# Column sums of the feed-forward and gate weights: other tiles than the ring of convolution accumulators

## The chip, the cores and the metric

The kernel runs on one core of a Trainium2 chip. The metric is the device time of one execution in microseconds (us). A core has five engines with their own instruction streams: TensorE (PE, matrix products; the loading of its weights is shown apart as PEld), VectorE (DVE), ScalarE (ACT), GpSimd (POOL) and SyncE (SP, which issues the transfers here). They wait for each other through semaphores. Tiles live in SBUF, results of PE in PSUM.

## The reference

A decoder layer on `x` of 16 sequences, 256 tokens, 512 features, all float32, in three blocks, each followed by a layer norm over the features:

1. A state-space block: RMS norm, one input projection to `z` (1024), `xi` (1024), `dt` (16), `B` and `C` (256 each); a causal depthwise convolution of four taps on `xi` and SiLU; the mean of `xi` in each of 16 heads; a linear recurrence over tokens with 16 states per head; a projection of its 16 outputs to 1024, gated by `silu(z)`; an output projection to 512 and the residual.
2. A long convolution: for each of 32 groups of 8 positions, products of `x` with a context are convolved with a kernel of 512 lags (in the reference by FFT), weighted with the context again and summed.
3. A feed-forward block: `base = x @ W.T + b`, plus a low-rank update of the two best of 8 experts, weighted by a softmax of gate logits `x @ gate_w.T + gate_b`.

What the change touches prepares block 3:

```python
base = x_flat @ W.T + b
logits = x_flat @ gate_w.T + gate_b
...
xA = jnp.einsum('nd,erd->ner', x_flat, lora_A)
...
out = base + SCALING * lora_update
```

The input of block 3 is a layer norm. The kernel multiplies weights whose column means have been subtracted with the input that is not yet normalised, so that the mean of the input drops out; the residual is in the weights too, as an added identity.

## The kernel before

The kernel has two parts. The first (blocks 1 and its norm) goes through 8 groups of 512 tokens, `g` from 0 to 7. The second (blocks 2 and 3) goes through 32 heads of positions. Instructions run on every engine in the order in which the program gives them; [...]the framework only adds the waits. A tile with a tag takes a slot in the ring of that tag; if all slots of the ring are held, the first writer of the new tile waits until the last reader of the slot's old tile is done.

In a group, ten pairs of output chunks of the input projections are computed one after another (`order`: `x`, `z`, `x`, `x`, `z`, `x`, `b`, `c`, `z`, `z`), each in seven half-size products (L328). Step `i` of the loop begins the products of pair `i` and ends those of pair `i-1`. After a pair of `xi` chunks is complete, `mixed` (L578 to L582) convolves its two chunks: the first tap of an even chunk on DVE (L580), of an odd chunk on ACT (L578), the three further taps on DVE (L582). The result is a tile with the tag `acc`, a ring of six slots of 128 x 512 float32; SiLU is applied in place later (L637). At `i == 6`, `head_means` (L593) multiplies the first four of these tiles into a PSUM tile `xm`.

PSUM tiles for various purposes share the tag `tr` with two banks: `xm`, the row `mw` of column means below, the outputs `yps` of the recurrence and others.

In group 1, between these steps, the weights of block 3, loaded at the end of group 0, are prepared: at `i == 2` DVE adds the identity to `w_f` (L518, L520); at `i == 3` POOL sums the four row blocks of `w_f` (512 columns), at `i == 4` those of `w_gl` (136 columns), both in `chunk_sum` (L525, L527); at `i == 5` and `i == 6`, `centred` multiplies a sum with a constant matrix on PE, which gives the column means in all partitions (L533), and DVE subtracts them from the four row blocks (L535):

```python
if g == 1 and i in (3, 4):
    w, cols = ((w_f, D), (w_gl, NE + ER))[i - 3]
    total = chunk_sum(w, cols)
if g == 1 and i in (5, 6):
    centred(*sums.pop(0))
```

In the kernel before, the two sums are tiles of the ring `acc`, beside the convolution's tiles.

Another ring is named here by the change: the tag `vn` of the pool `q3`, a single slot of 128 x 512 float32. In the first part it holds `yT`, the outputs of the recurrence, written by ACT near the end of each group (L700) and read by PE as weights (L735); in the second part it holds the loaded `vn` (L137 on). The pool `p1` has one slot for each of its tiles.

## Time and profile before

| | |
|---|---|
| median of 3 runs | 1436.82 us (1436.52 to 1436.96) |
| the profiled execution | 1436.9 us |
| its span, first to last instruction | 1435.1 us |
| mean granted clock of PE | 0.996 |
| PE busy | 1415.7 us (99% of the span) |
| DVE busy | 1209.7 us (84%) |
| ACT busy | 438.1 us (31%) |
| POOL busy | 470.6 us (33%) |
| chain that ended last | PE 96%, DVE 2%, issue 1%, POOL 1% |

Busy time is the sum over an engine's instructions; registers, branches and semaphores are not in it. The chain that ended last is followed back from the last instruction: at each step to what released it, or to the instruction before it on its engine. The granted clock is the share of PE's full rate that was let through. A time in a view is counted from the first instruction of the span; a line such as L535 is a line of the kernel before, and in the changed kernel lines from 525 on stand three lines further down.

### The profile page before, as it was taken

Reading aid. Unit: us, or ns where it says so; the run is one execution under the profiler, and the core shown is the slowest. Engines: PE = TensorE matmul, PEld = TensorE weight load, DVE = VectorE, ACT = ScalarE, POOL = GpSimd, SP = SyncE. Lnnn points to the kernel's source line nnn. Section 1 sums busy time; section 2 is a strip of 40 time slices with the busy share of each in tenths; the row PEclk is TensorE's granted clock in tenths of the full one; section 3 lists DMA queues with packets and bytes.
Section 4 is the critical chain, followed back from the end, with each engine's and each line's share of the span. In section 5 each row is a group of like instructions: output and inputs, shape, how many; then the busy total and the mean of one; then the engine's idle time right before and its main releaser. Section 6 shows DMA issues by size and latency. Waiting matters only on the chain.

```text
span 1435.1 us, 19011 instructions
## 1 busy us (share of the span) xinstructions
PE 1415.7 (99%) x6944; PEld 914.7 (64%) x6944; DVE 1209.7 (84%) x2102; ACT 438.1 (31%) x962; POOL 470.6 (33%) x661
## 2 busy tenths in 40 slices
PE   9999999999999999999999999999999999999997
PEld 7887788888888888888884444444444444444443
DVE  6988788878788787877847999999999999999996
ACT  2423223233232232332311333233323333333331
POOL 5452010010100201001003564556455545554552
PEclk9999999999999999999999999999999999999999
DMA  8114021120121111212003112221221122112200
GB/s 299 33 39 130 8 63 65 37 83 8 39 81 45 54 36 38 83 34 94 16 16 107 63 47 74 67 64 55 70 71 61 58 66 74 54 65 66 74 27 23
DMA packets 49166, 89.18 MB, mean 62 GB/s; under 512 B 8880, under 2 KB 13360, under 8 KB 49072
## 3 DMA queue, kind: packets, MB, share of 16 engines
q1 hardware_dynamic: 49072, 87.96, 19.2%
q8 instruction: 55, 0.90, 0.3%
q14 instruction: 39, 0.32, 0.1%
HBM read 70.62 MB, written 17.32 MB: 61 GB/s over the span
## 4 chain that ended last, share of the span: by engine, by line
PE 96%; DVE 2%; issue 1%; POOL 1%; DMA 0%; ACT 0%; POOLq 0%; SPq 0%; DVEq 0%
PE mm L328 20%; PE y L1021 15%; PE s L328 14%; PE y L1036 12%; PE base L1196 7%; PE s L778 6%; PE mm L778 6%; PE y L1006 4%; PE gl L1272 2%; PE base L1192 2%; PE tr L1108 1%; PE tr L145 1%; PE xm L593 1%; PE mm L735 1%; PE mm L869 1%; PE s L869 1%
## 5 line engine op out<-in xcount | busy, mean ns | idle before, releaser
L1071 DVE TENSOR_TENSOR pr<-y,cT 128x1024 f32<-128x1024 f32 x126 | 148.2, 1217 | 47.1 <-PE y L1036 47.1
L1036 PE MATMUL y<-kv 64*64 64x512 f32 x1536 | 179.6, 598 | 0.0
L582 DVE SCALAR_TENSOR_TENSOR acc<-xi,wc,acc 128x512 f32<-128x512 f32 x192 | 142.0, 753 | 9.8 <-ACT acc L578 4.1
L1081 DVE TENSOR_REDUCE red<-pr 128x128 f32<-128x1024 f32 x126 | 147.1, 1208 | 0.0
L155 DVE TENSOR_TENSOR kv<-tr,cT 128x1024 f32<-128x1024 f32 x124 | 145.4, 1213 | 0.0
L1021 PE MATMUL y<-kv 128*128 128x512 f32 x272 | 128.2, 594 | 0.6 <-ACT y L1010 0.4
L1036 PEld LDWEIGHTS y<-kv 64*64 64x64 f32 x1536 | 52.2, 132 | 119.0 <-issue 96.9
L1196 PE MATMUL base<-w_f,ol 128*128 128x512 f32 x248 | 121.4, 593 | 0.0
L1021 PE MATMUL y<-kv,Td 128*128 128x512 f32 x248 | 116.5, 592 | 0.0
L66 POOL TENSOR_TENSOR rs_a<-ve_a,nhalf 128x1 f32<-128x1 f32 x32 | 19.0, 594 | 243.0 <-DVE ve_a L64 243.0
L389 POOL TENSOR_TENSOR rstd<-ms,nhalf 128x4 f32<-128x4 f32 (+1 forms) x9 | 8.5, 948 | 258.9 <-DVE ms L387 258.9
L1021 PEld LDWEIGHTS y<-kv 128*128 128x128 f32 x272 | 51.1, 190 | 66.4 <-issue 48.9
L1229 POOL TENSOR_TENSOR ol<-o,red 128x512 f32<-128x512 f32 x31 | 39.4, 1272 | 161.7 <-DVE red L1081 161.7
L328 PE MATMUL mm<-XT,w_z 128*128 128x256 f32 x384 | 90.7, 379 | 0.0
L1021 PEld LDWEIGHTS y<-kv,Td 128*128 128x128 f32 x248 | 47.1, 190 | 59.3 <-issue 59.3
L991 POOL TENSOR_TENSOR xs<-kv 128x512 f32<-128x512 f32 x63 | 80.2, 1274 | 2.4
L1010 ACT COPY y<-y 64x512 f32<-64x512 f32 x124 | 69.2, 558 | 34.7 <-PE y L1006 28.9
L328 PEld LDWEIGHTS mm<-XT,w_z 128*128 128x128 f32 x384 | 73.0, 190 | 9.9
L328 PE MATMUL mm<-xnT,w_z 128*128 128x256 f32 x288 | 71.0, 382 | 0.0
L1006 PE MATMUL y<-xs,kv 128*128 128x512 f32 x124 | 64.8, 604 | 2.6 <-DVE pr L1071 1.6
L1196 PEld LDWEIGHTS base<-w_f,ol 128*128 128x128 f32 x248 | 42.5, 190 | 30.9 <-issue 30.9
L328 PE MATMUL s<-XT,w_xi 128*128 128x256 f32 x256 | 61.0, 380 | 0.6 <-DVE XT L224 0.5
(278 smaller groups left out, 2827.3 us busy)
## 6 DMA issues: line engine op xcount, KB each, us to landing
cT<-in_ctxT SPq DMA_DIRECT2D x32, 384.0 KB
kv<-in_toep SPq DMA_DIRECT2D x32, 384.0 KB
xt<-in_x SPq DMA_DIRECT2D x32, 256.0 KB
spread<-both SPq DMA_DIRECT2D x32, 256.0 KB
first<-xt SPq DMA_DIRECT2D x32, 256.0 KB
vn<-first SPq DMA_DIRECT2D x32, 256.0 KB
out<-res SPq DMA_DIRECT2D x31, 256.0 KB
xnT<-in_xT SPq DMA_DIRECT2D x7, 1024.0 KB
```

Source lines behind the costliest of these rows:

```text
L155: last = nc.vector.tensor_tensor(kv[:, q, k * BQ : (k + NL // 2) * BQ], vT[:, q, blks].rearrange("p k (b i) -> p (k b) i", i=NH).unsqueeze ...
L328: nc.tensor.matmul(ps, w[:, p, a, kc, :], Xs[b][:, kc, :], start=start and kc == 0, stop=stop and kc == 1, skip_group_check=upon,)
L582: ins = nc.vector.scalar_tensor_tensor(acc, xi[:, :, k : k + S], wc[:, c, k : k + 1], acc, ALU.mult, ALU.add)
L778: nc.tensor.matmul(ps, own[a][c][:, n * P : (n + 1) * P], w_o[b][c], start=start and c == 0, stop=stop and c == HC - 1, skip_group_check=upon,
L991: return nc.gpsimd.tensor_tensor(xs[:, q], moving(kv, q, 0), moving(kv, q, 1), ALU.add)
L1006: nc.tensor.matmul(bank_of(y, 3), T[:, SHARED_AT, :], xs[:, q], start=True, stop=True)
L1010: nc.scalar.copy(bank_of(y, 2)[b : b + HP], bank_of(y, 3)[a : a + HP])
L1021: nc.tensor.matmul(bank_of(y, lb), w, moving(kv, q, mb), start=not late and lb not in begun, stop=False, skip_group_check=True,)
L1036: return nc.tensor.matmul(bank_of(y, lb)[cols], T[rows, DIAGONAL_AT, (b - a) * HP : (b - a + 1) * HP], moving(kv, q, lb)[rows], start=star ...
L1071: nc.vector.tensor_tensor(pr.rearrange("p (k b j) i -> p k b j i", k=2, j=NH), y[i].rearrange("p k (b j i) -> p k b j i", j=NH, i=NH), cT[ ...
L1081: nc.vector.tensor_reduce(red[:, q, 2 * i : 2 * i + 2, :].rearrange("p k t -> p (k t)"), pr, AX.X, ALU.add)
L1196: nc.tensor.matmul(base, o_l[:, kc, :], w_f[:, kc, :], start=(first and kc == kcs[0]), stop=False)
```

## The change

`chunk_sum` no longer takes its tile from the ring `acc` of the pool `p2`. The sum of `w_f` (512 columns) becomes a tile of the one-slot ring `vn` in the pool `q3`, the sum of `w_gl` (136 columns) a tile of its own, `g_sum`, in the pool `p1`. Nothing else is edited.

```diff
         def chunk_sum(w, cols):
 
-            total = p2.tile([P, D], F32, tag="acc", name="w_sum", bufs=6)[:, 0:cols]
+            if cols == D:
+                total = q3.tile([P, D], F32, tag="vn", name="w_sum", bufs=1)
+            else:
+                total = p1.tile([P, cols], F32, name="g_sum")
             nc.gpsimd.tensor_tensor(total, w[:, 0, :], w[:, 1, :], ALU.add)
             for kc in range(2, KD):
                 nc.gpsimd.tensor_tensor(total, total, w[:, kc, :], ALU.add)
```

## The prediction

> **What bounds the kernel now.** I read the page's busy shares first: TensorE (PE) is busy 99% of the 1435.1 us span and the granted clock averages 0.996. A change that moves no matmul can therefore only win PE idle time or PE time at a lowered clock. The table of waits says where PE idle time is large enough to matter. In it, "A <- B: total, times, longest" means that A waited for B (first line from the whole span, the others from 100 to 175 us):

> ```profile
> PE xm L593 <- DVE w_f L535: 5.6, 1, 5.6
> ACT acc L578 <- PE mw L533: 5.7, 1, 5.7
> DVE acc L582 <- ACT acc L578: 2.3, 1, 2.3
> ```

> One single PE wait of 5.6 us, in token group 1. The chain that ended last, in order of time (start, us, what), shows how it arises:

> ```profile
> 140.80 0.25 PE mw L533 x2
> 141.05 0.02 issue
> 141.07 0.73 ACT acc L578
> 141.80 0.02 issue
> 141.82 0.77 DVE acc L582
> ...
> 144.15 2.40 DVE w_f L535 x4
> 146.55 0.04 issue
> 146.59 1.93 PE xm L593 x8
> 148.53 4.94 PE s L328 x16
> 153.47 6.04 PE mm L328 x28
> ...
> 240.78 1.00 PE xm L593 x8
> 241.78 3.65 PE s L328 x16
> 245.43 6.04 PE mm L328 x28
> ```

> Read upwards: the head means `xm` need a bank of the two-deep ring `tr`, which is held by the column mean of `w_f` until VectorE (DVE) has subtracted it (L535). L535 stands on DVE behind the convolution of chunk 5 (L582), whose first tap ScalarE (ACT) computes (L578). And that tap waited until the matmul on the sum of `w_gl` had read the ring slot the tap writes into. The DVE timeline (start, us, line, idle before it) prices the detour:

> ```profile
> 136.64 0.48 DVE L580 TENSOR_SCALAR acc<-xi,wc 128x512 f32<-128x512 f32 x1
> 137.15 2.33 DVE L582 SCALAR_TENSOR_TENSOR acc<-xi,wc,acc 128x512 f32<-128x512 f32 x3
> 141.82 2.33 DVE L582 SCALAR_TENSOR_TENSOR acc<-xi,wc,acc 128x512 f32<-128x512 f32 x3 [2.34 <-ACT acc L578]
> 144.07 2.47 DVE L535 TENSOR_TENSOR w_f<-w_f,mw 128x512 f32<-128x512 f32 x4
> ```

> The last view is busy time by stretch (PE first, PEclk in the third column from the right):

> ```profile
> 144.00:144.25 0.25, 0.00 (x0) 0.00 (x0) 0.25 (x2) 0.07 (x1) 0.00 (x0) 1.00 0.00 0
> 144.31:144.50 0.19, 0.00 (x0) 0.00 (x0) 0.19 (x1) 0.19 (x1) 0.00 (x0) 0.50 0.00 0
> 150.90:151.05 0.15, 0.15 (x2) 0.15 (x1) 0.00 (x0) 0.00 (x0) 0.00 (x0) 0.50 0.00 0
> 151.15:151.30 0.15, 0.15 (x2) 0.15 (x1) 0.00 (x0) 0.00 (x0) 0.00 (x0) 1.00 0.00 0
> ```

> So the stall has a second price: the clock is half from 144.28 to 151.11 us. In group 2 the matmuls from `xm` to the 28 `mm` take 245.43 - 240.78 = 4.65 us, in group 1 153.47 - 146.59 = 6.88. The halved clock costs 2.23 us after the stall's 5.6.

> **The change, part by part.** Times are of the profiled execution (1436.9 us, span 1435.1; the runs' median is 1436.82, 0.1 less). Instruction streams of both kernels are the same in number, kind and order on every engine and in the DMA queue; only waits differ.

> 1. *Work.* Three POOL additions for `w_f`, three for `w_gl`, two column-mean matmuls and eight subtractions stay as they are: 0.
> 2. *Taken away: the wait of chunk 5's tap.* Its input, `xi`, is ready at 136.31 + 0.41 = 136.72. The tap takes 0.72, so it is done at about 137.5. DVE gets to it after the three L582 of chunk 4. Six L582 in a row take 4.48 us where nothing stops them (130.19 to 134.67, the next start), so L535 starts at 137.15 + 4.48 = 141.63 instead of 144.07: 2.44 earlier. `xm` follows at 144.15 instead of 146.59. PE's stall falls from 5.56 (its timeline) to 3.12 us. It does not vanish: DVE itself, which has not been idle since 127.42 apart from this wait, is now what is late.
> 3. *Clock.* The window 140.87 to 144.28 still holds only 0.16 us of PE work before the stall and 0.13 after it, 8%, well below the 33% that lowered the clock elsewhere. I take it that the clock still falls at 144.28. But the window 144.28 to 147.69 is now full[...], so half clock lasts 3.41 us, not 6.83. The loss is 3.41 / 2 = 1.71 instead of 2.23: 0.52 more. The two unknowns, whether a window at 8% counts as idle and whether the next restores, bound this part between 0 and 3.41 us of loss, that is from +2.23 to -1.18.
> 4. *Waits moved.* Chunk 4's L580 loses a wait for PE that was over at 134.8, before 136.64: 0. The third and fourth subtraction of each weight now wait for POOL themselves, which was done at 128.85 + 1.02 = 129.9, 12 us earlier: [...]0.1 at most if two interruptions of L535's stream cost 0.05 each (successive operations overlap by about that). Behind them on DVE stand the sums of `x3`, whose PE consumer is at 153.31, so only `xm` would feel it. ACT's tap of chunk 3 (129.52) takes over a DMA wait that stood at the SiLU of chunk 2 (132.55, begun without idling). If that transfer landed only at 132.55 the tap ends 3.03 late; DVE needs it at 130.19 + 2.24 = 132.43, it was done at 130.24, so 2.19 is covered and 0.84 is the most it can cost. Traffic in that slot (the group's broadcast `rt`) was issued at 84.1, so 0.
> 5. *The new homes.* `w_sum` lies in the single slot `vn`, last read by L735 in group 0 at about 80 us, next written by ACT's `yT` at 173.86, 38 us after the mean matmul read it: 0 both ways. Cover would be gone only if one were 38 us later. `g_sum` is alone in its tile: 0.

> Does the gain last? From `xm` to `d_lg`, group 1 takes 195.55 - 146.59 = 48.96 and group 2 287.51 - 240.78 = 46.73; the difference is the 2.23 of clock and nothing else, so PE alone sets the pace, and `xnT` and `rt` loads are issued behind PE and DVE work that moves too. Sum: 2.44 + 0.52 = 2.96. Span 1432.1; time 1436.82 - 2.96 = 1433.86, rounded down to 1433.8 for the small early start inside the window.

> **Rivals.** *A: the clock is not lowered.* The stall is now shorter than a window (3.12 against 3.41), and if the windows fall differently in a run, no window is idle enough. Gain 2.44 + 2.23 = 4.67: 1432.15. Against it: the kernel before the stall is unchanged, and four executions within 0.44 us speak for a grid that falls alike each time. *B: one full window does not restore it,* or the grid cuts the shorter stall so that half clock lasts two windows after all. Half from 144.28 to 151.11 costs 3.41: gain 1.26, 1435.6; at the milder end the loss is as before and the gain 2.44, 1434.4. [...]against it: 147.69 to 151.11 restored at once. *C: the stall is held by something else,* L535 starting no earlier because chunk 5's tap has another late slot holder: 1436.8. Against it: the earlier holders of that ring were read by 104.3, when L778 had taken the last `z_sum`. *D, slower: the clock falls at the change of stages.* There PE idles from 770.0 to 771.67 and the window 768.92 to 772.33 is just 52% busy. The grid will stand about 3 us later against this work. If the share sank below the limit, somewhere from 33 to 52%, half clock would follow, and if it needs a full window to end, which none of the next four need be on the new grid, it covers their 2.99, 3.41, 2.64 and 3.29 us of PE work: up to 12.33 / 2 = 6.2 us lost, 1433.86 + 6.2 = 1440.0. Against it: sliding a window over that stretch, 52% is the least at any position.

> **How the numbers follow.** Chances: my forecast 0.62 (own range 1433.6 to 1434.1), A 0.15, B 0.13, C 0.05, D 0.05. About 0.2% is what a measurement of this kernel can tell from no change: below 1433.95 is faster, above 1439.7 slower. My forecast lies 0.1 us inside that border, so of its 0.62 I count 0.48 faster and 0.14 within; A adds to faster: 0.63. B and C are within: 0.32. D is slower: 0.05. The range 1432.0 to 1435.2 takes in the forecast, A and the milder half of B, above 0.8; C, D and B's far end are left out.

> **What would show it.** Right: ACT's tap of chunk 5 waits for DVE at about 136.8; no DVE idle between the six L582; L535 at 141.6; `xm` at 144.15 after 3.1 us of PE idle; half clock from 144.28 to 147.69; `mm` at 150.5; everything after group 1 shifted by 3.0. Wrong: `xm` still behind a PE-released tap (C), full clock throughout (A), half clock to 151.11 (B), a half clock near 770 us (D).

## The result and the profile after

The changed kernel takes 1433.1 us (median of 10 runs, 1431.64 to 1433.99), the kernel before 1436.55 (10 runs, 1435.55 to 1437.59). The ratio is 0.9975 with a 95% interval of 0.9967 to 0.9983: faster by 0.25%, inside the stated range, and 0.7 us faster than forecast. The profiled execution took 1433.19 us with a span of 1431.4, 3.7 less than the profiled execution before.

The same views as before. In the table of waits (100 to 175 us), PE's one large wait has shrunk, and the wait of ACT's tap for the column-mean matmul is no longer listed:

```profile
PE xm L596 <- DVE w_f L538: 3.1, 1, 3.1
```

The chain that ended last, in order of time (start, us, what), from 140.2 to 143.5 us:

```profile
140.21 0.75 DVE acc L585
140.97 2.40 DVE w_f L538 x4
143.37 0.04 issue
143.41 1.07 PE xm L596 x8
```

Before, the chain ran from the matmul `mw` over ACT's tap to DVE. Now it is DVE's own queue without a break, up to the subtraction. The timeline of DVE, and below it one line of ACT's (start, us, idle before in brackets):

```profile
135.89 0.48 DVE L583 TENSOR_SCALAR acc<-xi,wc 128x512 f32<-128x512 f32 x1
136.40 4.56 DVE L585 SCALAR_TENSOR_TENSOR acc<-xi,wc,acc 128x512 f32<-128x512 f32 x6
140.88 2.47 DVE L538 TENSOR_TENSOR w_f<-w_f,mw 128x512 f32<-128x512 f32 x4
```

```profile
136.00 0.72 ACT L581 ACTIVATE acc<-xi,wc 128x512 f32<-128x512 f32 x1 [1.34 <-DVE xi L372]
```

The six convolution steps run as one block of 4.56 us. The tap waits for its input alone and is done at 136.7, long before DVE wants it at 138.6. Last, busy time by windows: the stretches of 3.413 us into which the prediction divides the time between two changes of the clock. From the first change of this trace, at 7.81 us, to the fall at 144.34 it is 40 of them. PE stands first, PEclk third from the right:

```profile
140.93:144.34 3.41, 0.93 (x8) 0.16 (x8) 3.27 (x8) 0.63 (x1) 0.00 (x0) 1.00 0.00 0
144.34:147.76 3.42, 3.42 (x12) 2.73 (x9) 1.81 (x7) 0.96 (x2) 0.00 (x0) 0.50 0.00 0
147.76:151.17 3.41, 3.41 (x17) 3.00 (x17) 1.69 (x4) 0.76 (x2) 0.00 (x0) 1.00 0.00 0
```

Behind the window with 0.93 us of PE work (27%) the clock is half; behind the next, with 3.42 us of work in 3.42, it is full again. So half clock lasts 3.41 us (144.34 to 147.76) instead of 6.83.

The whole difference of the two executions is made by 196 us. Counted from the start of the `w_gl` mean matmul (140.64 before, 139.90 after), the head means start after 5.95 us before and 3.51 after: 2.44. From the head means to the next group's `d_lg` (195.48 and 191.77) it is 48.89 and 48.36: 0.53. The rest, 140.64 - 139.90 = 0.74, lies ahead of everything that the change touches: the first `d_lg` of group 0 already starts at 22.2 us before and 21.4 after, while the first sum is written at 124.16 and 123.42. Experiments 5 and 6 come back to it.

### The profile page after: what moved, and what is told of

It is laid out like the page before. It is cut to its first block, busy times and chain, and to the rows that moved or that the text cites. A ratio compares the mean times of both kernels' runs of the same rounds, so it can differ in the third digit from the quotient of the medians.

```text
span 1431.4 us, 19012 instructions
## 1 busy us (share of the span) xinstructions
PE 1414.3 (99%) x6944; PEld 913.6 (64%) x6944; DVE 1210.1 (85%) x2102; ACT 438.1 (31%) x962; POOL 470.0 (33%) x661
## 4 chain that ended last, share of the span: by engine, by line
PE 87%; DVE 2%; issue 1%; POOL 1%; ACT 0%; POOLq 0%; DVEq 0%
PE mm L328 16%; PE y L1024 15%; PE y L1039 12%; PE s L328 11%; PE base L1199 7%; PE s L781 5%; PE mm L781 5%; PE y L1009 4%; PE gl L1275 2%; PE base L1195 2%; PE tr L1111 1%; PE tr L145 1%; PE mm L738 1%; PE xm L596 1%; PE mm L872 1%; PE s L872 1%
## 5 line engine op out<-in xcount | busy, mean ns | idle before, releaser
L585 DVE SCALAR_TENSOR_TENSOR acc<-xi,wc,acc 128x512 f32<-128x512 f32 x192 | 141.9, 753 | 7.4 <-ACT acc L581 1.7
L328 PE MATMUL mm<-XT,w_z 128*128 128x256 f32 x384 | 90.7, 379 | 0.0
L328 PEld LDWEIGHTS mm<-XT,w_z 128*128 128x128 f32 x384 | 73.0, 190 | 9.9
L328 PE MATMUL mm<-xnT,w_z 128*128 128x256 f32 x288 | 71.0, 382 | 0.0
L328 PE MATMUL s<-XT,w_xi 128*128 128x256 f32 x256 | 61.0, 380 | 1.1 <-DVE XT L224 0.5
```

The costliest lines, as they stand in the source:

```text
L328: nc.tensor.matmul(ps, w[:, p, a, kc, :], Xs[b][:, kc, :], start=start and kc == 0, stop=stop and kc == 1, skip_group_check=upon,)
L585: ins = nc.vector.scalar_tensor_tensor(acc, xi[:, :, k : k + S], wc[:, c, k : k + 1], acc, ALU.mult, ALU.add)
```

## The experiments

**1 and 2. One sum at a time.** Which of the two sums made the wait? In `only_gate` the sum of `w_gl` alone leaves the ring, in `only_ff` that of `w_f` alone:

```diff
-            total = p2.tile([P, D], F32, tag="acc", name="w_sum", bufs=6)[:, 0:cols]
+            if cols == D:
+                total = p2.tile([P, D], F32, tag="acc", name="w_sum", bufs=6)
+            else:
+                total = p1.tile([P, cols], F32, name="g_sum")
```

> Only the sum of w_gl leaves the ring; the sum of w_f stays in it. Theory (the stall was lengthened by one late slot holder, the sum of w_gl, read at about 140.6 us): chunk 5's tap now takes the slot of the sum of w_f, which PE has read by about 134, before the tap's input is there at 136.7. Full gain: 1433.1 +- 0.6, PE idle before the head means 3.1 us, DVE without a gap between its six L585. Rival (both sums take slots and each counts, so that half the change brings half the gain): 1434.8, PE idle 4.3.

```diff
-            total = p2.tile([P, D], F32, tag="acc", name="w_sum", bufs=6)[:, 0:cols]
+            if cols == D:
+                total = q3.tile([P, D], F32, tag="vn", name="w_sum", bufs=1)
+            else:
+                total = p2.tile([P, D], F32, tag="acc", name="w_sum", bufs=6)[:, 0:cols]
```

> Only the sum of w_f leaves the ring; the sum of w_gl stays in it. Theory: chunk 5's tap still takes the slot of the sum of w_gl and waits for its column-mean matmul: no gain, 1436.5 +- 0.6, PE idle 5.6 us, DVE gap 2.3. Rival (each counts): 1434.8. Rival (the ring has one slot to spare as soon as either sum leaves): 1433.1.

Measured: `only_gate` 1433.7 us (1431.43 to 1435.06; ratio to before 0.9981, 0.9973 to 0.9990), `only_ff` 1436.17 (1435.64 to 1437.27; ratio 1.0000, 0.9992 to 1.0008). The waits from 100 to 175 us, of `only_gate` and of `only_ff`:

```profile
PE xm L596 <- DVE w_f L538: 3.1, 1, 3.1
```

```profile
ACT acc L581 <- PE mw L536: 5.7, 1, 5.7
PE xm L596 <- DVE w_f L538: 5.6, 1, 5.6
```

The sum of `w_gl` was the whole cause of the wait that the change removed. With `w_f`'s sum alone moved, chunk 5's tap waits 5.7 us for a PE matmul as in the kernel before and nothing is won. With `w_gl`'s alone moved, the stall is as short as with both. The rival that each sum counts for half is out. A gain from the new slot in the ring `vn` is not seen: `only_ff` is level with the kernel before, and the 0.6 us between the medians of `only_gate` and of the changed kernel are within the spread of their runs.

**3 and 4. The price of the clock.** Identity products, whose result is never read, keep PE busy during the stall. The first try had 28 of them:

```diff
                 if i == 6:
+                    if g == 1:
+                        ps = ps_s.tile([P, 512], F32, tag="s", name="s")
+                        for _ in range(28):
+                            nc.tensor.matmul(ps[:, 0:P], ident, ident, start=True, stop=True)
                     ms = [head_means(0)]
```

> The changed kernel with 28 products of the identity with itself (128 x 128, their result is never read) put into PE's stall before the head means in group 1, so that PE is busy while it waits. Theory (after a stall of 3.1 us the clock is halved for one window of 3.41 us, 1.71 us lost): the head means still start at the same time behind the subtraction, but at full clock throughout; 1433.1 - 1.7 = 1431.4. Rival (the slower matmuls after the stall are a refill of the pipeline and not the clock, or the idle time itself is all there is to win): 1433.1, or slower by what of the 28 products lasts beyond the subtraction.

Measured: 1434.72 us (1434.32 to 1435.53), slower than the changed kernel. I had counted 28 matmuls of 0.11 us; the chain has 56 for the 28 products, 6.25 us together, 0.112 each, so the head means started 146.21 - 139.64 = 6.57 us after the mean matmul instead of 3.51, 3.06 later. With 1.71 of clock time won back this is 1433.1 + 3.06 - 1.71 = 1434.45, near the measured time, but not a clean test. The same with `range(13)`:

> As the run with 28 identity products, but with 13: each of them runs as two passes of 0.112 us, so that 28 lasted 6.25 us, twice the stall, and 13 last 2.9, just inside the 3.1 us of it. Theory (the clock's window is a cost of its own behind the stall): head means start when they did in the changed kernel, full clock from the start on, 1433.1 - 1.7 = 1431.4 +- 0.5. Rival (no clock cost): 1433.1.

Measured: 1431.57 us (1431.01 to 1431.91). The PE timeline of `filled13`:

```profile
140.11 3.06 PE L662 MATMUL s<-ident 128*128 128x128 f32 x26
143.38 1.07 PE L596 MATMUL xm<-acc,mean 128*32 128x512 f32 x8 [0.21 <-DVE w_f L538]
144.38 1.13 PE L328 MATMUL s<-xnT,w_bc 128*128 128x256 f32 x4
```

The head means start 143.38 - 139.88 = 3.50 us after the mean matmul, as in the changed kernel. But the four products behind them take 1.13 us, where the changed kernel's take 2.08, and `d_lg` (190.10) follows after 46.72 us instead of 48.36: 1.64 less. The trace has no half clock between 7.66 and 1424.19 us. The whole kernel is 1.5 us faster by doing more. So the halved clock was a cost of its own here, beside the idle time: 0.95 us in these four products, 1.64 up to `d_lg`.

**5 and 6. The place of the windows.** The changed kernel, unedited, in two further executions:

> The changed kernel again, for the place of the clock's windows in another execution. Theory [...]: the first release after the start differs from 7.81 us; every change of the clock lies a whole number of windows after it; the stall of 3.12 us lowers the clock if one window overlaps it by 2.3 us or more, for one window if the next is full. Rival (windows start with the program): 7.81 us again.

> As the run before it: the changed kernel once more; the same theories with another place of the windows. Loss of clock time expected between 0 (stall split about evenly between two windows) and 1.7 us.

Measured: 1432.52 us and 1434.85 us, one execution each. The first release (the first change of the clock in a trace) is at 6.97 and 6.58 us, against 7.81 in the first profile of this kernel and 11.16 in the profile before. So it is not at a fixed time of the program. From the first release to the fall of the clock in group 1 it is 136.5 us in each of the three traces of this kernel, 40 windows (143.51 - 6.97, 143.11 - 6.58, 144.34 - 7.81), and 133.12 us in the kernel before, 39 windows. The expectation's 2.3 us of overlap was an estimate from the 33% in the trace of before: 3.41 x 0.67. The stall is 3.12 and 3.10 us, and in `again1` the clock is half from 143.51 to 146.92, one window. In `again2` it is half for two:

```profile
139.70:143.11 3.41, 0.86 (x5) 0.58 (x4) 3.37 (x6) 0.63 (x1) 0.00 (x0) 1.00 0.00 0
143.11:146.52 3.41, 2.85 (x10) 1.04 (x11) 3.16 (x10) 0.96 (x2) 0.00 (x0) 0.50 0.00 0
146.52:149.94 3.42, 3.42 (x9) 2.70 (x8) 0.00 (x0) 0.00 (x0) 0.00 (x0) 0.50 0.00 0
149.94:153.35 3.41, 3.41 (x17) 3.01 (x16) 1.86 (x4) 0.76 (x2) 0.00 (x0) 1.00 0.00 0
```

Here the first window, with 0.86 us of PE work (25%), is followed by half clock. The second, with 2.85 us (84%), is followed by half clock again; the third, full, by full clock. PE computes from 143.67 on at half clock until 149.94 and loses 6.27 / 2 = 3.1 us, more than the kernel before in its profile (2.23). A part of the second expectation fell with it: it put the loss at 1.7 at most. In `only_gate` full clock followed a window of 3.25 us of PE work, 95% (143.76 to 147.18), and at the start of `only_ff` the first release followed one of 3.04 us, 89% (3.15 to 6.56). On the other side, half clock followed more than the 33% of the trace of before: at the end of `filled13` it followed a window with 1.46 us of PE work, 43%:

```profile
1420.77:1424.18 3.41, 1.46 (x4) 0.43 (x3) 1.32 (x5) 0.98 (x2) 0.00 (x0) 1.00 0.08 31
```

The 52% at the change of stages (1.78 us, 768.92 to 772.33 before and 765.57 to 768.98 after) was followed by full clock. An estimate from the 43% and the 52% alone: a stall of 3.12 us would leave the clock full only where a boundary of the windows cuts it nearly in half, so that neither window has more than some 1.6 to 1.9 us idle.

The start of the kernel differs with the first release too. The timelines of PE, first of the kernel before, then of the changed one:

```profile
8.94 1.06 PE L395 MATMUL rt<-ident,rstd 128*128 128x128 f32 x4
9.79 1.71 PE L491 MATMUL mm<-ident 128*128 128x128 f32 x8
11.34 1.03 PE L328 MATMUL s<-xnT,w_xi 128*128 128x256 f32 x4
```

```profile
8.22 0.66 PE L395 MATMUL rt<-ident,rstd 128*128 128x128 f32 x4
8.71 1.06 PE L491 MATMUL mm<-ident 128*128 128x128 f32 x8
9.72 1.36 PE L328 MATMUL s<-xnT,w_xi 128*128 128x256 f32 x4
```

The same instructions take 1.06 and 1.71 us where the first release was at 11.16, and 0.66 and 1.06 where it was at 7.81; the first products start 1.6 us earlier, of which 0.74 are left at 140 us. That the rest went into waits for weights and sums at the start is only read from these timelines; it wasn't tried. Nor does the first release alone set the start: `again2`, released at 6.58, begins the mean matmul at 140.17, 0.27 later than the changed kernel's first profile, after a PE wait of 0.43 us for the transfer of `w_xi` at 10.16. So the cause of the 0.74 is not shown.

**7 and 8. What is left of the stall.** In `earlier`, the changed kernel's mean of `w_f` is taken and subtracted one step earlier; in `earlier_ring` the same is done to the kernel before, with both sums still in the ring of the convolution's tiles:

```diff
-                if g == 1 and i in (5, 6):
+                if g == 1 and i == 6:
                     centred(*sums.pop(0))
...
+                if g == 1 and i == 4:
+                    centred(*sums.pop(0))
                 if before is not None:
                     finish_products()
```

> The changed kernel with the column means of w_f taken and subtracted one step earlier, ahead of the sums of the second z pair and of the convolutions of chunks 4 and 5, so that the bank is free long before the head means ask for it. Theory (what is left of the stall is DVE's order: the subtraction behind two convolutions): PE idles about 0.4 us before the last products of that z pair and not before the head means; the clock stays full; 1433.1 - 3.1 - 1.7 + 0.4 = 1428.7. Rival (DVE is the bound of this stretch, so that moving its work only moves the stall): PE idles about 2.4 us elsewhere in group 1, 1431 to 1433.

> The kernel before, both sums still in the ring of the convolution's tiles, with the subtraction of the column means of w_f one step earlier. Theory (the late slot holder matters only while the head means stand behind chunk 5's convolution): chunk 5's tap still waits for PE until about 140.7, DVE idles 0.3 us or less for it, and PE does not idle before the head means: 1428.4 +- 0.4, as with the other tiles. Rival (the ring's wait costs its 2.4 us wherever the subtraction stands): 1430.9 or more.

Measured: `earlier` 1428.42 us (1427.86 to 1428.74; ratio to before 0.9944, 0.9931 to 0.9958), `earlier_ring` 1428.46 (1428.39 to 1428.76; 0.9945, 0.9931 to 0.9958). Both are 4.7 us faster than the changed kernel. The timelines of DVE, ACT and PE of `earlier_ring`:

```profile
134.05 2.47 DVE L535 TENSOR_TENSOR w_f<-w_f,mw 128x512 f32<-128x512 f32 x4
138.86 4.69 DVE L582 SCALAR_TENSOR_TENSOR acc<-xi,wc,acc 128x512 f32<-128x512 f32 x6
```

```profile
140.47 0.72 ACT L578 ACTIVATE acc<-xi,wc 128x512 f32<-128x512 f32 x1 [5.67 <-PE mw L533]
```

```profile
140.03 0.40 PE L533 MATMUL mw<-w_sum,share 128*128 128x136 f32 x2
140.36 1.07 PE L593 MATMUL xm<-acc,mean 128*32 128x512 f32 x8
```

ACT's tap still waits 5.67 us for PE, as in the kernel before. But the six convolution steps take 4.69 us with it and 4.56 without, and the head means follow the mean matmul at once. The ring's wait is the same and costs nothing, because nothing that PE needs stands behind it. So the change removed a wait that was only dear where the subtraction stood, and the place of the subtraction in DVE's order (its mean matmul moves with it) is worth more than the tiles: against the kernel before it brings 8.0 us, about the 5.56 us of stall and the 2.23 of clock together. The 0.4 us of PE idle that I expected before the last products did not come; the trace lists no PE wait for another engine from 100 to 250 us in `earlier`.

## Why the prediction was right

- *What bounds, and the wait removed (part 2).* Right to the hundredth: 2.44 us from the gap between the convolution steps, a stall of 3.12 us left, and DVE's queue as what is late next. Experiments 1 and 2 show the slot holder, 7 and 8 show DVE's order as the rest.
- *Clock (part 3).* Right in the profiled pair: 0.53 against 0.52, with a 27% window where I had 8%. That the two agree so closely is luck: the clock happened to fall at nearly the same time in these two executions (144.28 and 144.34 us). Experiment 4 shows the clock's price apart, about 1.5 to 1.6 us. That full clock would follow a full window was an estimate from the one in the trace of before (147.69 to 151.11); it came so behind 144.34 to 147.76. Wrong was the premise that the grid falls alike in each execution: its first release is at 7.81, 6.97 and 6.58 us in three executions of the changed kernel. The premise was taken from four executions that lay within 0.44 us. Ten runs of each kernel spread by 2.0 us before and 2.35 after. So the fall at 144.28 was not to be forecast, and the term is a spread, up to at least 3.1 us lost as in `again2`, not the single 0.52. The old stall has no fixed price either: the 5.56 us of it in `only_ff` were followed by (149.92 - 146.30) / 2 = 1.8 us of loss, not 2.23. One of the prediction's shares is a point off: 144.28 to 147.69 holds 1.10 us of PE work, 32%.
- *Waits moved and new homes (parts 4 and 5).* Right: `w_f`'s four subtractions take 2.47 us with the added waits as without, chunk 3's tap runs at 128.78 behind its input alone, and `only_ff` against before shows that the slot `vn` is free of cost.
- *The sum.* 2.96 forecast, 2.97 from the mean matmul to `d_lg` in the profiled pair, 3.45 between the medians. The difference of 0.5 is not settled. The spread of the windows is large enough for it, in the stall and at the start; `only_gate`, with the same stall, has a median 0.6 higher than the changed kernel. My own range of 1433.6 to 1434.1 was too narrow for the same reason; the wide one held.
- *Rivals.* A (full clock after the stall) was not seen in any of the four traces with the short stall, but it is not out. One of the ten runs, at 1431.64 us, has a mean granted clock of 0.999. Rounding allows it at most 4.3 us at half clock, and the end of the program alone took 3.1 to 5.6 us of that in the ten traces, so no room is left for a window of 3.41 us behind the stall. Two more of the ten runs lie within 0.11 us of it, in the range of `filled13`, which ran at full clock there; whether theirs was full too is not shown. B was seen once, in `again2`, by the second route that I had named, the grid. C is out: in the changed kernel and in `only_gate` the tap waits for its input alone, and DVE's gap is gone. D did not come: the window at the change of stages holds 52% again (765.57 to 768.98), and the clock stays full there.

## What to carry to other kernels

A ring slot's wait is priced at what stands behind the waiting instruction, not at its length (5.67 us of it cost nothing in `earlier_ring`): ask first whether the instruction that a busier engine needs can be put ahead of it. A stall of PE of 3.1 us cost up to as much again in clock here (0 to 3.1 us, the 0 argued from one run's mean clock), and that part varied with each execution, so a few microseconds of change want ten runs, not three. When two tiles leave a ring, look which one is read last; the other may be free to stay.

## What the hardware showed that I had not expected

The first release of the clock came at 6.56 to 11.16 us in six traces (6.56 in `only_ff`, 6.58 in `again2`, 6.97 in `again1`, 7.66 in `filled13`, 7.81 in the changed kernel's first profile, 11.16 before); in the five of them whose clock fell in group 1 it fell 40 windows of 3.413 us later, 39 before. Half clock followed even a window with 43% PE work (`filled13`). A stall of 3.1 us, shorter than one window, was followed by half clock for 3.41 us in three traces, and for 6.83 in one, where it held on behind a window with 84% PE work (`again2`). And 13 useless products in the stall made the kernel 1.5 us faster.
